# Turning the rows after the first norm by a transposing DMA instead of on TensorE, in an attention and ternary-FFN layer

## The chip, the cores and the metric

The kernel runs on one core of a Trainium2 chip. A core has five engines that run their own instruction lists in order and meet at semaphores: TensorE (PE, matrix products; its weight loads are shown as PEld), VectorE (DVE), ScalarE (ACT), GpSimd (POOL) and SyncE (SP), whose queue issues nearly all transfers here. Transfers run on 16 DMA engines. TensorE writes its results to PSUM; everything else works on SBUF, and DVE and ACT also read PSUM. The metric is the device time of one execution in microseconds (us).

## The reference

The layer takes `x` of 8 sequences of 1024 tokens with 512 features, and does linear attention with random features, a residual and a norm, then a layer with ternary weights, a residual and a norm:

```
def feature_map(x, orf):
    proj = x @ orf.T / d_k ** 0.25
    norm = jnp.sum(x * x, axis=-1, keepdims=True) / (2.0 * math.sqrt(d_k))
    return (jnp.exp(proj - norm) + EPS) / math.sqrt(m)
q = feature_map(split(x @ Wq.T + bq), orf)       # 16 heads of 32, 128 features each
k = feature_map(split(x @ Wk.T + bk), orf)
v = split(x @ Wv.T + bv)
kv = jnp.einsum('nlm,nld->nmd', k, v)
ksum = jnp.sum(k, axis=1)
...
out = out[..., :-1] / out[..., -1:]
x = _layernorm(x + out @ Wo.T + bo)              # the first norm
w_ternary = ste_quantize(weight)                 # -1, 0, 1
x = _layernorm(x + einsum('bsi,oi->bso', x, w_ternary * scale))
```

All is float32. The kernel keeps float32 accuracy from float16 matmuls by splitting a value into two float16 parts, a high part and the remainder.

## The kernel before, in words

The 8192 tokens go in 16 blocks of 512 (TB), two to a sequence; a block has four row tiles of 128 tokens (`tt`), and the 512 features have four groups of 128 (`kt` or `i`).

A block passes through these stages. `X` loads the transposed input (`xraw`) and splits it (`xh` on ACT, `xl` on DVE). `Stacked.project` makes k or q on PE, clamps it on DVE, and splits it on ACT and DVE into `part`; SP stores the parts to DRAM (`ds`) and loads them back in another layout (`st`, lines 576 and 577, and the norms `dn` to `st`, line 581). `KBlock.feature` multiplies `st_k` with the random features (`kf_ps`, line 630), ACT takes the exponent (`e`, line 635), POOL sums it, and PE accumulates `kvt`. `QBlock.feature` does the same for q (`qf_ps`, line 779); `products` makes numerator and denominator (`num_ps`, `den`, line 798, narrow matmuls into 32 output partitions each). The denominator (`rd` on ACT) goes to DRAM (`dd`, line 822), is inverted and is spread back (`r`, `dr`, `rb`). `divide` gives `oh` and `ol`, and `attn` multiplies them with Wo (`o_ps`, line 368).

Then comes the part that the change touches. For each row tile, `attn_add` (line 937, DVE) adds `o_ps` into the residual `y`; `layernorm` takes moments on DVE, the power on POOL, the shift on DVE, and applies both on ACT in place (line 904). `turn` (line 949) transposes the normed tile on PE, four float32 transposes of 128x128 into one PSUM tile `x_tp`. `x1_high` (line 953, ACT) reads that PSUM tile, scales it and writes the high float16 part `x1h`; `x1_low` (line 957, DVE) reads the PSUM tile and `x1h` and writes the remainder `x1l`. `ffn` (line 972) multiplies both parts with the ternary weights, eight matmuls to a row tile; `ffn_add`, the second norm and the store follow.

The order of the work is written out by hand. Class `Order` takes steps: a PE step has a place on a time axis and a length; a step of another engine has a delay behind a PE step (`after`) or a place (`at`); each lists what it needs. `emit` sorts all steps by the times that follow from this, lets narrow PE steps (`tiled`) be drawn together within a window, and issues the instructions in that order. Each engine then runs its own list in order, so places set nothing but the order on each engine; what waits is decided on the chip. The numbers in the code (`units`, the places of a block, the delays) are these places.

Buffers matter too: a tag with so many buffers is a ring, and a new tile waits until the last user of the tile that it replaces is done. PSUM tiles of tag `pj` have six buffers, `x1h` and `x1l` four each. Tag `t3`, three buffers of 2 KB a partition, holds `rd` of each block and, once per sequence, `kvt` and `kst`.

## Time and profile before

| What | Value |
|---|---|
| median of 3 runs | 1205.96 us (1203.72 to 1206.58) |
| the profiled execution's own time | 1203.99 us |
| its span, first to last instruction | 1202.1 us |
| granted TensorE clock | 0.997 of full speed |
| PE busy | 1174.0 us, 98% |
| DVE, ACT, POOL busy | 71%, 68%, 44% |
| DMA queue of SP | 166.24 MB, 48.2% of 16 engines |

Busy time is the union of an engine's instructions. PE's matmuls overlap, so the mean length of one is longer than the time from one start to the next; what a matmul costs PE is read from starts. In a group's line the part behind the bar is busy time and mean ns of one, and behind the second bar the engine's idle time just before and what ended it. In a line of the order of time the first number is the start, the second the length, and `x8` counts merged instructions. `SPq` is SP's queue, where the length is the time of issuing, not that of the transfer. In a table of stages the clock, the DMA engines' share and GB/s stand at the end of a line.

### The profile page before, as it was taken

To read this page: it belongs to the slowest core of one execution; us is meant where nothing else is said; L and a number is where in the kernel's file an instruction comes from. 1 tells how busy PE (TensorE), PEld (TensorE's weight loads), DVE (VectorE), ACT (ScalarE), POOL (GpSimd) and SP (SyncE) were. 2 spreads that over 40 slices of the span, in tenths; PEclk is the share of its full clock that TensorE was granted. 3 is DMA by queue.
4 is the path that set the end of the run, shared out by engine and by line. 5 is a ranking of instruction groups with operands and counts; after the bars stand their busy time and mean duration, and the time that the engine had idled before them with its cause. 6 is when DMAs were issued, how large, how long until landed. Compare 5 with 4: busy or idle time off the path is not lost.

```text
span 1202.1 us, 23702 instructions
## 1 busy us (share of the span) xinstructions
PE 1174.0 (98%) x8732; PEld 578.2 (48%) x8732; DVE 848.6 (71%) x1726; ACT 821.6 (68%) x1377; POOL 534.6 (44%) x485
## 2 busy tenths in 40 slices
PE   7899999999999999999999999999999999999996
PEld 4455454545445454554545445454544545445333
DVE  7886776776767676686766857578675776747488
ACT  4677686685766857676685766856677676857744
POOL 0357254615455253642527435273444625455323
PEclk9999999999999999999999999999999999999999
DMA  5556365453645436354454645536354453545621
GB/s 172 164 153 188 96 175 148 137 169 83 191 119 156 144 105 191 89 175 135 129 165 106 187 118 147 153 102 195 87 169 136 137 170 81 173 115 160 171 74 70
DMA packets 94819, 169.38 MB, mean 141 GB/s; under 512 B 14736, under 2 KB 48624, under 8 KB 92656
## 3 DMA queue, kind: packets, MB, share of 16 engines
q1 hardware_dynamic: 93296, 166.24, 48.2%
q10 hardware_dynamic: 1408, 1.63, 0.4%
q8 instruction: 69, 1.13, 0.4%
q14 instruction: 46, 0.38, 0.1%
HBM read 108.06 MB, written 59.77 MB: 140 GB/s over the span
## 4 chain that ended last, share of the span: by engine, by line
PE 85%; DVE 9%; ACT 3%; DMA 2%; issue 1%; POOL 0%; SPq 0%; ACTq 0%; POOLq 0%
PE q_ps L355 13%; PE v_ps L368 13%; PE k_ps L355 12%; PE o_ps L368 11%; PE f_ps L972 8%; PE kvt_ps L664 5%; PE kf_ps L630 5%; PE num_ps L798 5%; PE den L798 4%; PE qf_ps L779 4%; PE x_tp L949 2%; PE n_ps_k L545 1%; DMA y<-in_x_dram 1%; PE n_ps_q L545 1%; ACT qf L783 1%; DVE k_ps L497 1%
## 5 line engine op out<-in xcount | busy, mean ns | idle before, releaser
L647 POOL TENSOR_TENSOR esum<-esum,e 128x512 f32<-128x512 f32 x192 | 255.3, 1331 | 138.6 <-ACT e L635 130.8
L635 ACT ACTIVATE e<-kf_ps 128x512 f32<-128x512 f32 x256 | 149.8, 599 | 118.3 <-PE kf_ps L630 94.4
L783 ACT ACTIVATE qf<-qf_ps 128x512 f32<-128x512 f32 x256 | 141.6, 610 | 27.5 <-PE qf_ps L779 27.3
L928 POOL TENSOR_TENSOR y<-y,bo_sb 128x512 f32<-128x512 f32 x64 | 83.6, 1313 | 126.1 <-DMA y<-in_x_dram 58.5
L894 POOL TENSOR_TENSOR rs_a<-ve_a,neg_half 128x1 f32<-128x1 f32 x64 | 35.1, 548 | 194.8 <-DVE ve_a L889 172.6
L630 PEld LDWEIGHTS <-st_k 98*128 98x128 f16 x1024 | 75.9, 97 | 62.9 <-issue 12.9
L630 PE MATMUL kf_ps<-of,st_k 98*128 98x128 f16 x1024 | 96.2, 219 | 1.5 <-ACT e L635 1.2
L937 DVE SCALAR_TENSOR_TENSOR y<-o_ps,odown,y 128x512 f32<-128x512 f32 x64 | 47.9, 748 | 66.1 <-PE o_ps L368 65.5
L606 DVE SCALAR_TENSOR_TENSOR v<-v_ps,down_kqv,bv_sb 128x512 f32<-128x512 f32 x60 | 44.6, 744 | 62.3 <-PE v_ps L368 62.2
L779 PE MATMUL qf_ps<-st_q,of 98*128 98x512 f16 x256 | 82.2, 380 | 0.2
L368 PEld LDWEIGHTS <-oh 128*128 128x128 f16 x512 | 49.1, 97 | 67.0 <-ACT oh L871 7.3
L337 ACT ACTIVATE xh<-xraw,xup 128x512 f16<-128x512 f32 x64 | 45.2, 715 | 51.6 <-DVE xup L231 51.6
L355 PEld LDWEIGHTS <-wh_k 128*128 128x128 f16 x512 | 49.7, 99 | 59.7 <-issue 4.9
L510 DVE SCALAR_TENSOR_TENSOR rest_q<-q_ps,down_kqv,part_q 128x512 f32<-128x512 f32 x60 | 44.9, 748 | 46.7 <-ACT sq_q L505 44.6
L904 ACT ACTIVATE y<-y,mr_a,rs_a 128x512 f32<-128x512 f32 x64 | 52.4, 818 | 36.8 <-DVE mr_a L898 36.1
L618 POOL TENSOR_TENSOR vsum<-vsum,v 128x512 f32<-128x512 f32 x48 | 65.9, 1374 | 21.7 <-DVE v L606 21.6
L894 POOL TENSOR_TENSOR rs_f<-ve_f,neg_half 128x1 f32<-128x1 f32 x64 | 44.5, 695 | 67.8 <-DVE ve_f L889 63.4
L368 PEld LDWEIGHTS <-xh 128*128 128x128 f16 x512 | 48.5, 98 | 49.9 <-issue 3.4
L368 PE MATMUL o_ps<-wh_o,oh 128*128 128x512 f16 x256 | 67.1, 379 | 3.3 <-ACT oh L871 2.5
L355 PEld LDWEIGHTS <-wh_q 128*128 128x128 f16 x512 | 47.1, 97 | 45.5 <-issue 0.4
L368 PE MATMUL o_ps<-wh_o,ol 128*128 128x512 f16 x256 | 66.5, 378 | 2.0 <-DVE ol L876 2.0
L798 PE MATMUL num_ps<-qf,kv 128*32 128x512 f32 x512 | 67.4, 596 | 0.2
(216 smaller groups left out, 2715.0 us busy)
## 6 DMA issues: line engine op xcount, KB each, us to landing
ds_k<-part_k SPq DMA_DIRECT2D x128, 128.0 KB
st_k<-ds_k SPq DMA_DIRECT2D x64, 256.0 KB
ds_q<-part_q SPq DMA_DIRECT2D x128, 128.0 KB
st_q<-ds_q SPq DMA_DIRECT2D x64, 256.0 KB
rb<-dr SPq DMA_DIRECT2D x64, 256.0 KB
y<-in_x_dram SPq DMA_DIRECT2D x64, 256.0 KB
out_dram<-y SPq DMA_DIRECT2D x64, 256.0 KB
xraw<-in_xT_dram SPq DMA_DIRECT2D x15, 1024.0 KB
```

The lines of the kernel that those rows point to most:

```text
L355: nc.tensor.matmul(ps, a[:, kt, c], b[kt], start=(n == 0), stop=(n == 3 * KT - 1))
L368: nc.tensor.matmul(ps, a[kt][:, c], wt[:, kt, :], start=(n == 0), stop=(n == 3 * KT - 1))
L618: nc.gpsimd.tensor_tensor(sums["v"], sums["v"], vs[tt], op=ALU.add)
L630: nc.tensor.matmul(ps[:, j, :], self.st[i][0:NF, j, c], of, start=True, stop=True)
L635: nc.scalar.activation(e, self.eps[i, tt], AF.Exp, scale=EXP_SCALE)
L647: nc.gpsimd.tensor_tensor(es, before, self.es[i, tt].rearrange("p j m -> p (j m)"), op=ALU.add)
L779: nc.tensor.matmul(self.qps[n], of, self.st[i][0:NF, j, :], start=True, stop=True)
L783: nc.scalar.activation(e, self.qps[n], AF.Exp, scale=EXP_SCALE)
L798: nc.tensor.matmul(to[DK * j : DK * (j + 1), :], kvl[:, n, i * P + DK * j : i * P + DK * (j + 1)], self.qf[i, j], start=first, stop=last, ...
L894: nc.gpsimd.tensor_tensor(self.rs[name], self.ve[name], neg_half, op=ALU.pow)
L928: nc.gpsimd.tensor_tensor(y, y, bo_sb, op=ALU.add)
L972: nc.tensor.matmul(ps, a[:, kt, :], tern.w[:, kt, :], start=(n == 0), stop=(n == 2 * KT - 1))
```

## The change

The turned float16 parts are made in another order. After the norm is applied, `x1_high` and `x1_low` split the row tile `y` itself, in SBUF, into the two halves of a tile `x1p` (128 x 2 x 512, float16, tag `t3` with its three buffers). SP then issues one transposing DMA for the tile, which writes `x1t` (128 x 8 x 128, four buffers). `ffn` reads the eight 128x128 pieces of `x1t`. The four transposes on PE and the PSUM tile are gone. `turned` is no longer a PE step with a place of its own: it hangs behind the output's PE step with delays, called from `output`.

Nearly all other places and delays in the order also have new numbers, without changing what is computed.

```
-        def turn(self, tt):
-            self.tps[tt] = pj.tile([P, KT, P], F32, tag="pj", name=f"x1_tp_{self.t}_{tt}")
-            for kt in range(KT):
-                nc.tensor.transpose(self.tps[tt][:, kt, :], self.y[tt][:, kt * P : (kt + 1) * P], ident)
-        def x1_high(self, tt):
-            self.x1h[tt] = sb.tile([P, KT, P], F16, tag="x1h", name=f"x1h_{self.t}_{tt}", bufs=4)
-            nc.scalar.mul(self.x1h[tt], self.tps[tt], X1_SCALE)
-        def x1_low(self, tt):
-            xl = sb.tile([P, KT, P], F16, tag="x1l", name=f"x1l_{self.t}_{tt}", bufs=4)
-            nc.vector.scalar_tensor_tensor(
-                xl, self.tps[tt], X1_SCALE, self.x1h[tt], op0=ALU.mult, op1=ALU.subtract
-            )
-        def turned(self, tt, place):
-            step = pe(place, 0.45, self.turn, tt, needs=[self.a_gates[tt]])
-            high = after(step, 2.07, self.x1_high, tt)
-            self.x1_gates[tt] = after(step, 5.07, self.x1_low, tt, needs=[high])
+            self.turned(tt, step)                      # at the end of output
+        def x1_high(self, tt):
+            self.x1p[tt] = sb.tile([P, 2, D], F16, tag="t3", name=f"x1p_{self.t}_{tt}", bufs=3)
+            nc.scalar.mul(self.x1p[tt][:, 0, :], self.y[tt], X1_SCALE)
+        def x1_low(self, tt):
+            pair = self.x1p[tt]
+            nc.vector.scalar_tensor_tensor(
+                pair[:, 1, :], self.y[tt], X1_SCALE, pair[:, 0, :], op0=ALU.mult, op1=ALU.subtract
+            )
+        def turn(self, tt):
+            self.x1t[tt] = sb.tile([P, 2 * KT, P], F16, tag="x1t", name=f"x1t_{self.t}_{tt}", bufs=4)
+            nc.sync.dma_start_transpose(self.x1t[tt], self.x1p[tt].rearrange("p a d -> p (a d)"))
+        def turned(self, tt, step):
+            high = after(step, 2.06, self.x1_high, tt, needs=[self.a_gates[tt]])
+            low = after(step, 9.26, self.x1_low, tt, needs=[high])
+            self.x1_gates[tt] = after(step, 3.37, self.turn, tt, needs=[low])
...
-            for a in self.x1t[tt]:
+            for a in range(2):
                 for kt in range(KT):
-                    nc.tensor.matmul(ps, a[:, kt, :], tern.w[:, kt, :], start=(n == 0), stop=(n == 2 * KT - 1))
+                    nc.tensor.matmul(ps, self.x1t[tt][:, KT * a + kt, :], tern.w[:, kt, :], start=(n == 0), stop=(n == 2 * KT - 1))
...
-    units = [0.0, 51.61, 104.67, 168.51]
+    units = [0.0, 51.61, 104.84, 168.05]
...
-        k.norms(a + k0 + (19.92 if t > 2 else 3.7))
+        k.norms(a + k0 + (16.46 if t > 2 else 2.9))
...
-        y, r, m, d, f = u + -5.46, u + 13.45, u + -5.65, u + 12.58, u + 42.82
-        ys, rs, ms, fs, ds = 6.01, 0.05, 5.86, 5.63, 2.42
+        y, r, m, d, f = u + -4.0, u + 9.12, u + -5.65, u + 14.73, u + 42.82
+        ys, rs, ms, fs, ds = 5.43, 1.72, 5.86, 5.08, 3.06
...
-            f = E + (45.81, 87.24, 112.69)[n]
+            f = E + (44.62, 85.21, 115.19)[n]
```

## The prediction

> **What bounds the kernel now.** I read the page's engine shares first, then the table of stages, then the groups with shapes kept apart, then the order of time on PE and on SP's queue in one steady block.
>
> The page's first part, and the table of stages (us; then PE, PEld, DVE, ACT, POOL busy with counts; clock; DMA share; GB/s):
>
> ```profile
> PE 1174.0 (98%) x8732; PEld 578.2 (48%) x8732; DVE 848.6 (71%) x1726; ACT 821.6 (68%) x1377; POOL 534.6 (44%) x485
> ...
> q1 hardware_dynamic: 93296, 166.24, 48.2%
> ```
> ```profile
> 180.00:1102.00 922.00, 919.20 (x6947) 452.36 (x6945) 637.56 (x1285) 642.17 (x1082) 427.52 (x379) 1.00 0.49 140
> ...
> 1162.00:1202.00 40.00, 29.20 (x146) 14.36 (x144) 33.89 (x86) 18.39 (x27) 12.62 (x18) 0.94 0.14 53
> ```
>
> From 180 to 1102 us PE is idle 2.8 us in 922, at full clock: what leaves PE's list there shortens the kernel, if nothing new makes PE wait. In the last 40 us PE is busy 29 and DVE 34; the chain of waits there is mostly DVE (moments, the two adds, x1l). PE work that leaves there is worth nothing; DVE work added there costs its length.
>
> Groups by shape (busy us, mean ns of one | idle before): the removed transposes, the two splits that move, and the nearest rows for what they become.
>
> ```profile
> L949 PE MATMUL x_tp<-ident,y 128*128 128x128 f32 x256 | 36.7, 273 | 0.1
> L957 DVE SCALAR_TENSOR_TENSOR x1l<-x_tp,x1h 128x512 f16<-128x512 f32 x64 | 42.6, 681 | 6.5 <-ACT x1h L953 6.4
> L953 ACT ACTIVATE x1h<-x_tp 128x512 f16<-128x512 f32 x64 | 37.8, 629 | 1.1 <-PE f_ps L972 1.1
> L343 DVE SCALAR_TENSOR_TENSOR xl<-xraw,xup,xh 128x512 f16<-128x512 f32 x64 | 59.2, 933 | 2.0 <-ACT xh L337 2.0
> L876 DVE TENSOR_TENSOR ol<-num,oh 128x512 f16<-128x512 f32 x64 | 46.8, 739 | 4.8 <-ACT oh L871 4.8
> L871 ACT CAST oh<-num 128x512 f16<-128x512 f32 x64 | 39.6, 621 | 27.3 <-DVE num L866 27.2
> L337 ACT ACTIVATE xh<-xraw,xup 128x512 f16<-128x512 f32 x64 | 45.2, 715 | 51.6 <-DVE xup L231 51.6
> ```
>
> Order of time in block 11, PE (start us, length): where eight transposes stand, and what follows them.
>
> ```profile
> 771.61 1.04 PE L949 MATMUL x_tp<-ident,y 128*128 128x128 f32 x8
> 772.58 1.06 PE L798 MATMUL num_ps<-qf,kv 128*32 128x512 f32 x8
> 773.46 1.04 PE L798 MATMUL den<-qf,kv 128*32 128x512 f32 x8
> ...
> 775.18 1.04 PE L798 MATMUL den<-qf,kv 128*32 128x512 f32 x8
> 776.15 0.62 PE L630 MATMUL kf_ps<-of,st_k 98*128 98x128 f16 x8
> 776.61 0.61 PE L949 MATMUL x_tp<-ident,y 128*128 128x128 f32 x4
> 777.05 0.39 PE L630 MATMUL kf_ps<-of,st_k 98*128 98x128 f16 x4
> ```
>
> Matmuls overlap, so starts count: four transposes from 776.61 to 777.05 take 0.44 us, 109 ns each, not the mean of 273. Before a narrow (128*32) group eight take 0.97 instead of 0.87: entering narrow work costs 0.10. Between narrow groups eight take 0.86 to 0.88, but the last before kf_ps 0.97: leaving costs another 0.10.
>
> SP's queue in the same block:
>
> ```profile
> 767.67 0.33 SPq L562 DMA_DIRECT2D dn_k<-n_k  x1
> 773.17 0.25 SPq L581 DMA_DIRECT2D st_k<-dn_k  x1
> 773.52 0.50 SPq L576 DMA_DIRECT2D st_k<-ds_k  x1
> ...
> 774.70 0.27 SPq L581 DMA_DIRECT2D st_k<-dn_k  x1
> ...
> 780.35 0.34 SPq L827 DMA_DIRECT2D r<-dd  x1
> 785.38 0.34 SPq L837 DMA_DIRECT2D dr<-r  x1
> 786.85 1.72 SPq L843 DMA_DIRECT2D rb<-dr  x4
> ```
>
> One issue holds SP 0.25 to 0.6 us, and between issues SP sits waiting. This is the room that the new transfers get.
>
> **The change, part by part.**
>
> *Transposes leave PE.* 64 turns of four, 0.436 us each: 27.9 us. Eight turns start after 1162, in the DVE-bound tail, and count nothing. The other 56 give −24.4 (ends −24.4 and −27.9). 64 PSUM tiles go too; PE hardly waits for PSUM (0.1 us before x_tp), so nothing for that.
>
> *PE's new order.* In the built programs PE's list has 74 stretches of narrow matmuls before and 93 after. 19 more at 0.10 + 0.10 = +3.9 us (down to +2 if half of the borders fall where PE waits anyway).
>
> *The split moves ahead of the turn.* x1_high now reads y in SBUF: 621 (oh) to 715 (xh) ns for 629; ACT gets −0.5 to +5.5 us in all, at 68% busy, covered by PE. x1_low reads SBUF twice: 739 (ol, same shapes, one operation less) to 933 (xl, the same two operations) for 681. I take 933: DVE +16 us in all, 0.25 each, covered at 71% busy. In the tail eight of them are not covered: +2 (low end +0.5). If DVE's cover went, the 16 us would appear, less the tail's 2.
>
> *The transposing DMA, 64 of 256 KB, all on SP's queue.* No row shows one. As bytes it adds 16.8 MB to 166.2 MB: the 48.2% share of the DMA engines becomes 53%. At the page's rate (166.24 MB in 48.2% of 1202 us, 287 GB/s) one takes 0.9 us of the DMA engines and, like a plain 256 KB load, 0.5 us of SP. The other end: the instruction as built moves blocks of 16 rows, so a partition gets 32 bytes of a block; if each such piece cost a mean packet (0.482 x 16 x 1202 us over 93296 packets, 99 ns), one takes 8192 / 16 x 99 ns = 51 us, and 64 take 3.2 ms. The ends lie far apart; I take the plain 256 KB load as the nearest row, because the transfer moves whole rows of one tile, doubled for caution: about 2 us of SP and of the rings.
>
> Where it stands: in a steady block SP's list now reads x1t_0, three loads of st_k_1, x1t_1, x1t_2, st_k_2, x1t_3, st_k_3, the stores of dd. Each x1t waits for x1_low on DVE, and all of that queues behind it. Who waits: kf_ps on PE for st_k. In the block shown st_k_1's last load is issued at 774.70 and its first matmul starts at 781.40; st_k_0's last load, at 773.17, is read at 776.15, so about 3.0 us suffice to land and 3.4 us are spare. st_k_2 and st_k_3 have 10 us more and over (read at 792.9 and 802.7). k's norms also move 3.5 us earlier, which puts st_k_0 ahead of x1t_0. The consumer has the most room: f_ps starts 16 to 24 us after x1l's end in steady blocks (771.3 to 787.3 and the like). ACT gets one real new wait: x1p shares three buffers with rd, so x1p_3 waits for x1t_0's landing, and rd for x1t_1's. The applies of rows 0 and 3 are 11.3 us apart (763.86, 775.19): x1t_0 has some 9 us. At 2 us all of this is covered: 0. In the tail the last rows' f_ps came 0.4 to 1.0 us after x1l; now a landing lies between. By dd to r (last dd issued by 778.52, r at 780.35) that is 1.8 us or more; DVE has other rows' work meanwhile: +1 (0 to +4).
>
> *New places elsewhere* (SP, ACT, POOL and DVE lists all reshuffled). PE idles 28 us in all, 10.8 of them in the last 40, about 11 in the first 60, under 4 between 60 and 1102. There is little to win and I take −4, with ends −8 and +8.
>
> Sum: −24.4 + 3.9 + 2 + 0 + 1 − 4 = −21.5. The profiled execution took 1203.99 us (span 1202.1, 1.9 around it), 2.0 below the median of 1205.96. So 1182.5, and 1184 against the median.
>
> [...]
>
> **The rivals.**
>
> *Hidden (likeliest), 0.56.* 1184, own range 1172 to 1197.
>
> *The transposes back up SP's queue: slower, 0.31.* SP's waits in the block shown, 768.0 to 773.17, 780.7 to 785.38 and 788.57 to 792.79, with st_k_1's 3.4 us, are about 17 to 18 us of room for four: it decides from 4.5 us of queue per transpose. Beyond it st_k comes late, kf_ps waits, ACT stalls in x1p_3, and each further us costs four times in some 14 blocks, 56 us. At 5 us 1212, at 6 us 1268, at 7 us 1324; at 51 us over 4 ms. For it: nothing in the trace moves data in 2-byte steps, and SP waited 5.2 us for one 256 KB store (767.67 to 773.17), so the rings are not idle. Against: SP's small room is needed only if the price is nine times a plain issue.
>
> *Hidden, but the gain is eaten, 0.13.* DVE's uncovered part (14), the worse places (+8) and landings in the tail (+4) together give back 10 to 26: 1194 to 1210. For: 19 more narrow stretches. Against: DVE at 71%.
>
> **How the numbers follow.** 0.3% (3.6 us) is about what a measurement of this kernel can tell from no change. Faster: 0.56 and 0.05 of the last, 0.61. Same: 0.05. Slower: 0.31 and 0.03, 0.34. Range: below, the hidden case with all 27.9 and places −8, 1170. Above, up to 6.1 us per transpose, 1275, which leaves about 0.15 above it and 0.02 below.
>
> **What would show it.** Right: no x_tp on PE; PE busy near 1150; 64 issues x1t<-x1p on SP of 2 us or less; kf_ps waiting for st_k no more than now; x1p ahead of x1t by one DVE step; DVE x1l near 0.93 us; the last f_ps 2 to 4 us behind their x1l. Wrong: issues or landings of x1t over 4.5 us, PE waiting for st_k or f_ps for x1t in every block, ACT idle before x1p_3 or rd.

## The result and the profile after

The changed kernel takes 1215.33 us (median of 4 runs, 1212.36 to 1215.76), the kernel before on the same chip 1204.90. The ratio is 1.008, with a 95% interval of 1.0058 to 1.0102: 10 us slower, where 21.5 us less were forecast. The profiled execution has a span of 1213.9 us.

Three lines of the page of the changed kernel: busy time by engine, packets, and SP's queue.

```profile
PE 1161.1 (96%) x8476; PEld 549.2 (45%) x8476; DVE 865.7 (71%) x1726; ACT 832.2 (69%) x1377; POOL 529.7 (44%) x485
...
DMA packets 162402, 186.14 MB, mean 153 GB/s; under 512 B 82320, under 2 KB 116208, under 8 KB 160240
...
q1 hardware_dynamic: 160880, 183.03, 61.3%
```

The 256 transposes have left PE's list (8732 to 8476), and 16.8 MB more cross SP's queue, as forecast. The queue's packets went up by 67,584, that is 1056 for each of the 64 transfers, most of them of 256 bytes, and its share of the DMA engines went from 48.2% to 61.3%. Worked out: (0.613 x 1213.9 - 0.482 x 1202.1) / 64 = 2.6 us of all 16 engines for one transfer.

The stages of the changed kernel (us; PE, PEld, DVE, ACT, POOL busy; clock; DMA share; GB/s):

```profile
60.00:180.00 120.00, 111.54 (x986) 56.41 (x975) 78.45 (x137) 83.29 (x140) 58.38 (x45) 0.97 0.48 138
180.00:1102.00 922.00, 909.42 (x6707) 427.92 (x6705) 653.11 (x1279) 653.99 (x1086) 426.04 (x382) 1.00 0.65 155
1102.00:1162.00 60.00, 54.61 (x371) 21.73 (x368) 41.83 (x87) 40.05 (x70) 18.00 (x20) 0.97 0.66 166
1162.00:1214.00 52.00, 36.00 (x152) 14.70 (x152) 42.22 (x107) 22.74 (x32) 16.49 (x21) 0.90 0.50 122
```

PE's idle time between 180 and 1102 us is 12.6 us, where it was 2.8; between 60 and 180 us it is 8.5, where it was 0.5 in the kernel before:

```profile
60.00:180.00 120.00, 119.47 (x1035) 60.36 (x1024) 87.81 (x145) 91.04 (x154) 63.36 (x47) 1.00 0.53 153
```

The changed kernel's groups with shapes kept apart:

```profile
L953 DVE SCALAR_TENSOR_TENSOR x1p<-y,x1p 128x512 f16<-128x512 f32 x64 | 45.8, 715 | 0.3 <-ACT x1p L949 0.3
L949 ACT ACTIVATE x1p<-y 128x512 f16<-128x512 f32 x64 | 40.3, 630 | 3.2 <-DMA x1t<-x1p 1.2
L630 PE MATMUL kf_ps<-of,st_k 98*128 98x128 f16 x1024 | 97.2, 219 | 16.4 <-DMA st_k<-ds_k 8.0 <-DVE x1p L953 4.5 <-DMA st_k<-dn_k 1.7
```

The two splits are cheap in SBUF. The new wait is that of `kf_ps` (16.4 us idle ahead of it). From block 3 to block 14 it comes once in a block, at the first `kf_ps`, which reads `st_k_0` (0.1 us in block 5, 0.5 to 1.9 us in the others); where the view names `x1p` or another tile of DVE, it is the same place. Block 11 of the changed kernel in order of time, first SP's queue, then PE (start, length):

```profile
771.70 0.51 SPq L301 DMA_DIRECT2D xraw<-in_xT_dram  x1
772.32 0.50 SPq L576 DMA_DIRECT2D st_k<-ds_k  x1
772.87 0.57 SPq L577 DMA_DIRECT2D st_k<-ds_k  x1
774.99 0.26 SPq L581 DMA_DIRECT2D st_k<-dn_k  x1
775.29 0.54 SPq L527 DMA_DIRECT2D ds_k<-part_k  x1
775.92 2.99 SPq L960 DMA_TRANSPOSE x1t<-x1p  x1
...
781.33 4.39 SPq L960 DMA_TRANSPOSE x1t<-x1p  x2
```
```profile
783.16 0.38 PE L630 MATMUL kf_ps<-of,st_k 98*128 98x128 f16 x4 [1.05 <-DMA st_k<-ds_k]
```

`st_k_0` was asked for at 772.32 and 772.87, ahead of the block's first transpose at 775.92, and at 783.16 PE has waited 1.05 us for it. The issue of one transpose takes SP 1.23 us at the least, 1.82 on the mean over all 64, and 2.99 here.

The records of packets and landings tell what happens meanwhile. A spill `ds_k` lands in four parts, 5.2 to 5.9 us behind its issue (medians of 128; one more record comes at 1.0 us), where a load of `st_k` lands in 16. Around 770.5 us, where little else runs, four or five packets, all of 1024 bytes, are under way at a time. Both are read here as a spill on 4 of the 16 DMA engines. From 780 to 782.5 us at least 16 packets are under way all the time, yet only 0.03 to 0.04 MB move in each half microsecond. Beside the packets of a spill and a few of 4 and 8 KB these are 256-byte packets of the transpose, 18 ns long at the median; 16 of them last over 1 us, up to 4.2, and end together at 782.9. Of the 16 landings of `st_k_0`'s second load four come between 779.59 and 781.52, and twelve between 782.95 and 783.03, right behind that end.

So it is in each of the twelve blocks from 3 to 14: 15 to 20 long packets of the transpose end together, `st_k_0`'s last part lands 0.1 to 0.5 us later, and `kf_ps` starts within 0.13 us of that. The waits at these twelve places add up to 11.7 of the 16.4 us. Over all 64 transposes the 16 landings of one lie within 0.15 us of each other at the median. For a plain copy of the same bytes (`e3_plain_copy` below) they lie 2.8 us apart. These records look as if the parts of a transpose waited for each other, and a load that was issued ahead waited with them. What holds either, no run shows.

A gap of PE can have a price of its own. Two stretches of the changed kernel around a wait of 3.62 us for ACT (columns as above), and PE's line:

```profile
172.40:176.00 3.60, 0.04 (x4) 0.04 (x6) 1.25 (x2) 1.21 (x3) 0.00 (x0) 0.99 0.97 260
176.00:179.40 3.40, 3.40 (x15) 1.20 (x16) 3.40 (x6) 3.03 (x6) 1.81 (x1) 0.51 0.69 199
```
```profile
175.96 0.65 PE L664 MATMUL kvt_ps<-e,v 128*32 128x128 f32 x8 [3.62 <-ACT e L635]
```

After the gap the granted clock is 0.51 for 3.4 us, which costs, as an estimate from these two numbers, some 1.7 us more. The same follows a wait of 1.98 us that ends at 100.0. It does not follow every wait: behind one of 1.90 us that ends at 495.9 the clock stays up. Between 60 and 1180 us the changed kernel has four such stretches, the kernel before none.

### The profile page after: what moved, and what is told of

Read it like the earlier page. It is cut to its first block, busy times and chain, and to the rows that moved or that the text cites. A ratio compares the mean times of both kernels' runs of the same rounds, so it can differ in the third digit from the quotient of the medians.

```text
span 1213.9 us, 23180 instructions
## 1 busy us (share of the span) xinstructions
PE 1161.1 (96%) x8476; PEld 549.2 (45%) x8476; DVE 865.7 (71%) x1726; ACT 832.2 (69%) x1377; POOL 529.7 (44%) x485
## 3 DMA queue, kind: packets, MB, share of 16 engines
q1 hardware_dynamic: 160880, 183.03, 61.3%
## 4 chain that ended last, share of the span: by engine, by line
PE 77%; DVE 11%; DMA 7%; ACT 2%; issue 1%; POOL 1%; SPq 1%; POOLq 0%; DVEq 0%; ACTq 0%
PE q_ps L355 12%; PE v_ps L368 11%; PE k_ps L355 11%; PE o_ps L368 11%; PE f_ps L972 8%; PE kf_ps L630 4%; PE kvt_ps L664 4%; PE num_ps L798 4%; DMA st_k<-ds_k 4%; PE den L798 4%; PE qf_ps L779 3%; PE n_ps_k L545 1%; PE n_ps_q L545 1%; DMA rb<-dr 1%; DVE num L866 1%
## 5 line engine op out<-in xcount | busy, mean ns | idle before, releaser
L647 POOL TENSOR_TENSOR esum<-esum,e 128x512 f32<-128x512 f32 x192 | 251.4, 1313 | 154.9 <-ACT e L635 152.2
L783 ACT ACTIVATE qf<-qf_ps 128x512 f32<-128x512 f32 x256 | 146.4, 603 | 32.5 <-PE qf_ps L779 32.0
L972 PE MATMUL f_ps<-tern,x1t 128*128 128x512 f16 x512 | 128.7, 379 | 1.3 <-DMA x1t<-x1p 0.5
L894 POOL TENSOR_TENSOR rs_a<-ve_a,neg_half 128x1 f32<-128x1 f32 x64 | 41.3, 646 | 180.7 <-DVE ve_a L889 180.6
L630 PE MATMUL kf_ps<-of,st_k 98*128 98x128 f16 x1024 | 97.2, 219 | 16.4 <-DMA st_k<-ds_k 8.0
L779 PE MATMUL qf_ps<-st_q,of 98*128 98x512 f16 x256 | 88.1, 382 | 2.5 <-DVE st_f L885 1.5
L618 POOL TENSOR_TENSOR vsum<-vsum,v 128x512 f32<-128x512 f32 x48 | 62.0, 1292 | 30.0 <-DVE xm L210 17.0
L972 PEld LDWEIGHTS <-x1t 128*128 128x128 f16 x512 | 47.3, 98 | 61.3 <-issue 8.1
L504 ACT ACTIVATE part_k<-k_ps,bk_sb,down_kqv 128x512 f16<-128x512 f32 x60 | 46.9, 782 | 35.0 <-DVE k_ps L497 25.8
```

What stands on the lines that cost most here:

```text
L618: nc.gpsimd.tensor_tensor(sums["v"], sums["v"], vs[tt], op=ALU.add)
L630: nc.tensor.matmul(ps[:, j, :], self.st[i][0:NF, j, c], of, start=True, stop=True)
L647: nc.gpsimd.tensor_tensor(es, before, self.es[i, tt].rearrange("p j m -> p (j m)"), op=ALU.add)
L779: nc.tensor.matmul(self.qps[n], of, self.st[i][0:NF, j, :], start=True, stop=True)
L783: nc.scalar.activation(e, self.qps[n], AF.Exp, scale=EXP_SCALE)
L894: nc.gpsimd.tensor_tensor(self.rs[name], self.ve[name], neg_half, op=ALU.pow)
```

## The experiments

The theories of the first round were: A, the new places cost the time; B, the transposing DMA does. In several kernels x1 stays unturned or sums are left incomplete, so that a cost can be taken out; each is named where it comes. "Old" and "new" places are those of the kernel before and of the changed kernel.

### Each part alone

`e1_old_places` is the kernel before, with the new splits and the transposing DMA hung behind the output step:

```
             self.a_gates[tt] = self.layernorm(step, last, tt, f"a_{self.t}_{tt}")
+            self.turned(tt, step)
...
-            q.turned(tt, d + ds * tt + 15.51)
```

> The transposing DMA and the split ahead of it as in the changed kernel, but every other step at the place it had in the kernel before. Theory A (the new places cost the time: the longer start-up, kf_ps waiting at 93 to 176 us, and the tail; the transposing DMA itself is as good as hidden): the 25 us less of PE work come through, 1180 to 1190 us. Theory B (the transposing DMA costs the time: it holds SP's queue and all 16 DMA engines in front of st_k's loads, and kf_ps waits in every block): 1205 to 1220 us, with kf_ps waiting for st_k some 1 to 2 us per block at the old places too.

Measured: 1236.3 us, ratio 1.0275 (1.0238 to 1.0313). Neither theory: the old places make it worse. The waits of this kernel that stand out (us in total, times, longest):

```profile
ACT x1p L949 <- DMA x1t<-x1p: 15.1, 11, 3.2
PE kvt_ps L664 <- ACT e L635: 13.4, 13, 2.4
```

Here the ring of three `x1p` fills: ACT waits for a landing of `x1t` before it may write the next `x1p`, and what stands behind it in ACT's list, `e`, comes late for PE. `e6_spread_old_places` below shows that this is not all: there the wait for `x1t` is gone and that of `kvt_ps` is not.

`e2_new_places` keeps the transposes on TensorE and puts all else at the new places:

```
-            self.turned(tt, step)
...
+            q.turned(tt, d + ds * tt + 15.51)
```

> The transposes on TensorE and the split behind them as in the kernel before, with every other step at the places of the changed kernel. Theory A (places): PE's work is back (+25) and the places' waits stay (some 11 us before 180 us, some 10 in the last 100): 1222 to 1236 us. Theory B (transposing DMA): the places are worth nothing much either way, 1200 to 1212 us, and the waits of kf_ps for st_k in the steady blocks are gone.

Measured: 1267.6 us, ratio 1.0521 (1.05 to 1.0543), far outside of both. The turns on PE need places of their own, which the new places don't have, and the ones chosen here may be bad ones. So this run doesn't price the new places. It does say that the numbers of an order belong to one list of work.

### The transposing DMA, step by step

`e3_plain_copy` moves the same bytes with a plain DMA, and `e11_no_dma` lets the splits write into `x1t` itself. In both x1 is not turned, and the second matmul of a block reads unturned rows.

```
-            nc.sync.dma_start_transpose(self.x1t[tt], self.x1p[tt].rearrange("p a d -> p (a d)"))
+            nc.sync.dma_start(self.x1t[tt].rearrange("p a d -> p (a d)"), self.x1p[tt].rearrange("p a d -> p (a d)"))
```
```
-            self.x1p[tt] = sb.tile([P, 2, D], F16, tag="t3", name=f"x1p_{self.t}_{tt}", bufs=3)
+            self.x1t[tt] = sb.tile([P, 2 * KT, P], F16, tag="x1t", name=f"x1t_{self.t}_{tt}", bufs=4)
+            self.x1p[tt] = self.x1t[tt].rearrange("p (a k) d -> p a (k d)", a=2)
...
-            self.x1_gates[tt] = after(step, 3.37, self.turn, tt, needs=[low])
+            self.x1_gates[tt] = low
```

> The changed kernel with a plain DMA of the same 256 KB from x1p to x1t in place of the transposing one; x1 is not turned, so the second matmul of the block multiplies the unturned rows. Theory A (places): nothing changes, 1210 to 1217 us. Theory B (what is costly is the transposing form: 1.24 us of SP each, 1024 packets of 256 bytes, all 16 engines held until the slowest is through): the 14 us that the steady blocks lost come back and part of the tail's, 1194 to 1202 us, and kf_ps waits for st_k in the steady blocks no more than before (under 0.5 us per block).

> The changed kernel with no DMA between x1p and x1t: the two splits write into x1t itself, and x1 is not turned. Spills on 4 engines. It gives the time without any transfer. Theory C: like the plain copy or a little below it, 1190 to 1200 us; what is then left above 1182 us (the 25 us less of PE work) is the new places' own. Theory A in its weaker form (the places also cost some 20 us): 1200 to 1210 us.

Measured: 1202.1 us (ratio 0.9977, 0.9963 to 0.9992) and 1202.2 us (0.9986, 0.9966 to 1.0005). A plain copy of 256 KB a row tile costs nothing that these runs can tell; the transposing form costs 13 us. Theory C's range for the kernel without any transfer, 1190 to 1200 us, is missed: it lies where the weaker form of theory A put it, so the transposing DMA is not all that keeps the kernel from the forecast 1184 us. The wait of `kf_ps` without any DMA falls from 16.4 to 5.2 us:

```profile
L630 PE MATMUL kf_ps<-of,st_k 98*128 98x128 f16 x1024 | 97.0, 218 | 5.2 <-DMA st_k<-dn_k 3.3 <-ACT e L635 0.9 <-DVE x1t L954 0.8
```

`e4_spread_after` is the changed kernel with spills that land in 16 parts. The DRAM tile gets the shape of the SBUF tile, so that the outermost dimension of the store is 128 and not 4, and the load takes the new layout apart. The loads thereby become three in place of two, and no run parts this from the stores:

```
-                self.ds[i] = dram.tile([2, DK, HPT, TB], F16, tag="ds", name=f"ds_{self.which}_{self.t}_{i}")
-            nc.sync.dma_start(self.ds[i][r].rearrange("d j t -> j d t"), self.part[i][:, r, :])
+                self.ds[i] = dram.tile([2, P, TB], F16, tag="ds", name=f"ds_{self.which}_{self.t}_{i}")
+            nc.sync.dma_start(self.ds[i][r], self.part[i][:, r, :])
...
-            ds = self.ds[i].rearrange("r d j t -> (r d) j t")
-            nc.sync.dma_start(st[0 : 2 * DK], ds)
-            nc.sync.dma_start(st[2 * DK : 3 * DK], ds[DK : 2 * DK])
+            for n, r in enumerate((0, 1, 1)):
+                nc.sync.dma_start(st[n * DK : (n + 1) * DK], self.ds[i][r].rearrange("(j d) t -> d j t", d=DK))
```

> The changed kernel with k's and q's spilled parts stored from 128 partitions in a layout that reaches all 16 DMA engines, where the present store uses 4 of them, and loaded back in three loads of 32 partitions. Theory A (places): little changes, 1208 to 1218 us. Theory B in the form that a transposing DMA waits on the 4 engines that hold the spills' backlog, and holds the other 12 meanwhile: without the backlog kf_ps no longer waits for st_k in the steady blocks, 1196 to 1206 us. Theory B in the form that the issue on SP alone delays the loads: no change, or slower by the third load's issue (0.5 us on SP for each of 128 stacks, covered or not): 1212 to 1225 us.

Measured: 1194.02 us, ratio 0.991 (0.9895 to 0.9925). This is 21 us less than the changed kernel and 11 less than the kernel before. Between 180 and 1102 us PE is busy as it was before the change, and `kf_ps` no longer waits for its loads:

```profile
180.00:1102.00 922.00, 919.36 (x6836) 434.42 (x6838) 672.56 (x1315) 663.19 (x1103) 432.32 (x387) 1.00 0.63 159
```
```profile
L629 PE MATMUL kf_ps<-of,st_k 98*128 98x128 f16 x1024 | 97.0, 218 | 1.2 <-ACT e L634 0.9 <-DVE ve_a L888 0.3
```

The old spills, with an outermost dimension of 4, land in four parts, the spread ones, with 128, in 16.

Four more kernels part the spread from the transposing DMA. `e5_spread_before` has the same spread in the kernel before, `e10_plain_spread` has it with the plain copy (x1 unturned), `e16_spread_k_only` has it for k alone, and `e18_no_dma_spread_k` for k alone with no DMA (x1 unturned). In the two for k alone both pairs of lines above are chosen by

```
+            ds = self.ds[i][r] if self.which == "k" else self.ds[i][r].rearrange("d j t -> j d t")
+            nc.sync.dma_start(ds, self.part[i][:, r, :])
```

> The kernel before with the spills stored from 128 partitions over all 16 DMA engines, as in the run that took the changed kernel to 1194 us. Theory C (only a transposing DMA suffers from spills that sit on 4 engines, because it holds the other 12 until these are through): in the kernel before, where kf_ps did not wait for st_k, nothing is won, 1200 to 1208 us. Theory D (spills on 4 engines cost time in either kernel): 1183 to 1192 us, and the gain of the spread says nothing about the transposes.

> The changed kernel with spread spills and with a plain DMA from x1p to x1t in place of the transposing one (x1 is not turned). Theory C: without a backlog the transposing form costs little more than a plain copy, 1188 to 1194 us against 1194 us. If the form itself (1.24 us of SP, 1024 packets of 256 bytes) costs time without a backlog too: 1175 to 1186 us.

> The changed kernel with only k's spills spread over 16 engines; q's keep their 4 engines and their two loads. The transposes stand on SP's queue between k's spills and st_k's loads, q's spills come some 30 us after them. If the backlog of k's spills is what the transposes wait on: all of the gain is here, 1188 to 1196 us, and with 64 loads fewer than with both spread perhaps a little below its 1194 us. If the spread helps for another reason (shorter stores, or loads in other pieces, for k and q alike): about half of the gain, 1202 to 1208 us.

> The changed kernel with no DMA between x1p and x1t (1202 us), with k's spills spread over 16 engines. If k's spills hinder the new places also without any transposing DMA: 1192 to 1197 us, the same as with the transposing DMA and the same spread (1196.8), so that the transfer costs nothing there. If the spread only undoes what the transposing DMA suffers: 1200 to 1204 us.

Measured: 1211.2 (ratio 1.0046, 1.0032 to 1.006), 1195.3 (0.9911, 0.9893 to 0.9929), 1196.8 (0.9928, 0.9912 to 0.9945) and 1197.2 us (0.9932, 0.9917 to 0.9947). The kernel before gains nothing from the spread and loses 6 us, so theory D falls; it lies above theory C's range (1200 to 1208) as well, and what loses the 6 us was not looked into. In the changed kernel the spread of k alone gives 18.5 of the 21 us. With it, the transposing DMA (1196.8) costs no more than no DMA at all (1197.2), and with both spread no more than a plain copy (1194.0 against 1195.3). Theory C holds in this: the 13 us exist only together with k's spills in the old layout, which land in four parts. The spread also gives the new places 5 us without any transfer, which C did not say.

`e12_act_queue` issues the transposes from ACT's queue:

```
-            nc.sync.dma_start_transpose(self.x1t[tt], self.x1p[tt].rearrange("p a d -> p (a d)"))
+            nc.scalar.dma_start_transpose(self.x1t[tt], self.x1p[tt].rearrange("p a d -> p (a d)"))
```

> The changed kernel with the transposes issued from ACT's queue in place of SP's; spills on 4 engines. Theory C says that what costs is that a transpose stands behind the spills in the order of one queue and st_k's loads behind it. From another queue its packets need not wait for the spills, nor st_k's loads for it: kf_ps waits for st_k under 5 us in all (16 us by line in the changed kernel), 1196 to 1208 us, ACT's 64 issues of 1.24 us included as far as PE covers them. If it is the DMA engines themselves that are held, whatever the queue, kf_ps waits as before and ACT's 79 us of issues come on top: 1215 to 1250 us.

Measured: 1266.4 us, ratio 1.0498 (1.0457 to 1.0539). From the page and the groups of this kernel:

```profile
q1 hardware_dynamic: 93296, 166.24, 47.9%
q10 hardware_dynamic: 68992, 18.42, 11.0%
```
```profile
L630 PE MATMUL kf_ps<-of,st_k 98*128 98x128 f16 x1024 | 100.8, 224 | 4.7 <-DMA st_k<-dn_k 1.9 <-ACT sq_q L505 1.5 <-ACT e L635 0.9
L779 PE MATMUL qf_ps<-st_q,of 98*128 98x512 f16 x256 | 93.8, 394 | 37.6 <-ACT num L810 22.8 <-ACT qf L783 13.7 <-DMA st_q<-dn_q 0.8
```

Half of what C expects is there: from a queue of their own the transposes leave `kf_ps` 4.7 us of idle time and not 16.4. But ACT now issues each transpose itself, 1.43 us on the mean, behind DVE's `x1p`, and `qf_ps` is idle 37.6 us, 36.5 of them for ACT. The time lies outside of both ranges, so this run tells only where the wait of `kf_ps` comes from.

### The old places with the DMA

> The transposing DMA at the old places (1236 us), with the spills over 16 engines. There ACT's x1p waited 15 us for landings of x1t (11 times), and PE's kvt_ps and v_ps for ACT's e behind it (25 us). Theory C (the landings are late because the transposes wait behind the spills' backlog): the waits go, 1178 to 1195 us. Theory E (the rows come too close together there for a ring of three x1p shared with rd, whatever the DMA engines hold): ACT's wait for x1t stays over 10 us, 1215 to 1236 us.

`e6_spread_old_places` is `e1_old_places` with the spread. Measured: 1221.2 us, ratio 1.0128 (1.0105 to 1.0151). ACT's wait for `x1t` goes from 15.1 to 1.3 us, as theory C says; PE's wait of `kvt_ps` for `e` stays at 12.1 us (13.4 in `e1_old_places`), so the time doesn't follow. It falls into theory E's range, but without E's wait: neither theory explains it.

`e19_old_splits` and `e20_old_splits_spread_k` put the splits at their old places too, and the DMA right behind them:

```
+        def turned(self, tt, place):
+            high = at(place + 2.07, self.x1_high, tt, needs=[self.a_gates[tt]])
+            low = at(place + 5.07, self.x1_low, tt, needs=[high])
+            self.x1_gates[tt] = at(place + 5.08, self.turn, tt, needs=[low])
```

> The old places for every step, the two splits too (they read y in SBUF), and the transposing DMA directly behind the low part. x1p is held some 4 us before its DMA, not 7 as with the changed kernel's delays at the old places (1236 us). Spills on 4 engines. If holding x1p in a ring of three was what made ACT wait there: 1195 to 1210 us, less the better the hold of the DMA engines is hidden. If the transposing DMA hurts at the old places in any case: 1215 to 1240 us.

> The same with k's spills spread over 16 engines. If old places, short hold and spread spills together keep what the removed PE work is worth: 1180 to 1192 us, faster than the changed kernel with the spread (1194). If the gain at the old places is small anyway: 1194 to 1210 us.

Measured: 1258.6 (ratio 1.0422, 1.0381 to 1.0464) and 1246.0 us (1.0327, 1.03 to 1.0354). Both lie outside of their ranges. A shorter hold of `x1p` is no cure; ACT still waits 11.8 and 20.4 us for `x1t`, and `f_ps` now waits 9.5 and 7.7 us for it as well. Why the old places carry the DMA so badly stays open.

### What the transposes on PE were worth

`e17_turn_removed` is the kernel before without the transposes, and with nothing in their place: the splits read `y` at the places that the order had given them, and x1 is not turned.

```
-            step = pe(place, 0.45, self.turn, tt, needs=[self.a_gates[tt]])
-            high = after(step, 2.07, self.x1_high, tt)
-            self.x1_gates[tt] = after(step, 5.07, self.x1_low, tt, needs=[high])
+            high = at(place + 2.07, self.x1_high, tt, needs=[self.a_gates[tt]])
+            self.x1_gates[tt] = at(place + 5.07, self.x1_low, tt, needs=[high])
...
-            q.turned(tt, d + ds * tt + 15.51)
+            q.turned(tt, d + ds * tt + 15.96)
```

> The kernel before with the transposes on TensorE left out and nothing in their place: the two splits read y in SBUF, at the places that they had; x1 is not turned. It gives what 27.9 us less of PE work are worth with the old places. If the prediction's first step was right (24.4 us of it on the path): 1178 to 1184 us. If much of it was not on the path, because PE then runs into waits for other engines that the transposes had covered: 1190 to 1200 us.

Measured: 1203.86 us, ratio 0.999 (0.998 to 0.9999), above both ranges. All transposes are gone, nothing replaces them, and 1.5 us are won. In block 11 of the kernel before, the eight transposes stood between the last six `qf_ps` and the `num_ps` and `den` which read what ACT makes of them. Its order of time, the line of PE ahead of those shown in the prediction, and ACT's:

```profile
770.31 1.46 PE L779 MATMUL qf_ps<-st_q,of 98*128 98x512 f16 x6
```
```profile
770.79 3.04 ACT L783 ACTIVATE qf<-qf_ps 128x512 f32<-128x512 f32 x6
773.67 1.15 ACT L953 ACTIVATE x1h<-x_tp 128x512 f16<-128x512 f32 x2
```

And the same piece of both lists without the transposes:

```profile
768.35 1.46 PE L779 MATMUL qf_ps<-st_q,of 98*128 98x512 f16 x6
769.74 1.35 PE L798 MATMUL num_ps<-qf,kv 128*32 128x512 f32 x8
770.63 1.33 PE L798 MATMUL den<-qf,kv 128*32 128x512 f32 x8
771.49 1.65 PE L798 MATMUL num_ps<-qf,kv 128*32 128x512 f32 x7
772.52 0.63 PE L798 MATMUL den<-qf,kv 128*32 128x512 f32 x3
772.97 0.59 PE L798 MATMUL num_ps<-qf,kv 128*32 128x512 f32 x1
772.97 1.44 PE L798 MATMUL den<-qf,kv 128*32 128x512 f32 x5
774.35 0.84 PE L630 MATMUL kf_ps<-of,st_k 98*128 98x128 f16 x12
```
```profile
767.34 0.62 ACT L948 ACTIVATE x1h<-y 128x512 f16<-128x512 f32 x1
...
768.91 2.55 ACT L783 ACTIVATE qf<-qf_ps 128x512 f32<-128x512 f32 x5
771.29 0.69 ACT L948 ACTIVATE x1h<-y 128x512 f16<-128x512 f32 x1
771.81 0.65 ACT L783 ACTIVATE qf<-qf_ps 128x512 f32<-128x512 f32 x1
```

From the first of the six `qf_ps` to the `kf_ps` behind the group it was 770.31 to 776.15, 5.84 us, with eight transposes in it; it is 768.35 to 774.35, 6.00 us, without them. `num_ps` and `den` stretch from 3.57 us (772.58 to 776.15) to 4.61, because they wait for ACT: the last `qf` ends at 772.46, and the `num_ps` that reads it starts at 772.51.

Two causes are mixed in these 1.04 us. One is cover: in the kernel before, PE worked off transposes while ACT caught up. The other is that this run also changed ACT's list: without the PE step that they had hung behind, two `x1h` now stand ahead of the last `qf`, where the kernel before had both behind it. Counted from the first of the six `qf_ps`, the last `qf` ends 3.52 us later in the kernel before and 4.11 us later here. These 0.59 us are ACT's own delay, and by this estimate the cover is the other 0.45. All twelve groups of this kind between 180 and 1102 us are longer by 1.04 to 1.18 us, and all have two `x1h` ahead. A run with the `x1h` kept behind `qf` would part the two causes; there is none.

The waiting can be counted over the whole kernel. For each pair of neighbouring matmuls the start-to-start time that such a pair takes at the lower quartile in the kernel before stands for PE at work, and the rest is waiting. PE at work falls by 27 to 30 us, by how the narrow matmuls are grouped, and the waiting rises by as much. Between 180 and 1102 us some 13 us of the rise lie at `num_ps` and `den`, and some 10 at `kvt_ps`, which reads ACT's `e`.

DVE slowed down too. The group of `xl` in this kernel, 933 ns on the mean in the kernel before:

```profile
L343 DVE SCALAR_TENSOR_TENSOR xl<-xraw,xup,xh 128x512 f16<-128x512 f32 x64 | 70.1, 1104 | 0.0
```

By its overlap with POOL in the trace, `xl` takes 745 ns on the mean where POOL is idle, and 1355 ns (741 to 1821) where POOL is busy for over 90% of it; 36 of 64 fall into the second kind, where 18 did in the kernel before. Why it takes longer beside POOL, no run shows. To see what this is worth, `e21_removed_less_pool` cuts most of POOL's adds to 64 of 512 columns, which leaves the sums of e incomplete, and `e22_before_less_pool` does the same to the kernel before.

```
+            if self.half == 1 or tt > 1:
+                es, before, new = es[:, 0:64], before[:, 0:64], new[:, 0:64]
```

> The old places with the transposes left out (1203.9 us), and 160 of POOL's 192 adds of e cut from 512 columns to 64, so that POOL is busy far less; the sums of e are not complete. Theory F: at the old places the gain is lost because PE's shorter list shifts DVE's two-input instructions onto POOL's work, where each takes 1.1 to 1.4 us and not 0.68 to 0.74 (xl 933 to 1104 ns on the mean, DVE 39 us more in all), and PE then waits for what ACT and DVE make. With POOL mostly quiet the gain must come out: 1178 to 1190 us, xl near 800 ns. If the gain is lost for another reason: 1198 to 1206 us.

> The kernel before with the same cut of POOL's adds, for comparison. PE is busy 98% there and idle some 6 us between 60 and 1102 us, so a faster DVE has little to give: 1198 to 1206 us by either theory. If this falls as far as the other run, the cut and not the removed transposes is what is seen there.

Measured: 1198.5 (ratio 0.9944, 0.9929 to 0.9959) and 1204.8 us (0.9997, 0.9987 to 1.0006). `xl` falls to 793 ns, as theory F expects:

```profile
L343 DVE SCALAR_TENSOR_TENSOR xl<-xraw,xup,xh 128x512 f16<-128x512 f32 x64 | 50.3, 793 | 0.0
```

But only 5.4 us come back, against some 20 that F asks for, and the waiting at `kvt_ps` falls by as much. F is a part. The 13 us at `num_ps` and `den` are unchanged in this run.

The old places are not those of the changed kernel, and there the loss lies elsewhere. The start of block 4's first `kf_ps`, the time from there to that of block 14, and the rest, in the profiled executions:

| us | up to block 4 | ten blocks | from block 14 on |
|---|---|---|---|
| before | 271.4 | 722.8 | 207.9 |
| `e17_turn_removed`, old places, no transposes | 272.8 | 718.4 | 211.0 |
| `e11_no_dma`, new places, no transfer | 273.4 | 713.1 | 212.3 |
| `e18_no_dma_spread_k`, the same, k's spills spread | 271.2 | 708.9 | 214.7 |
| `e16_spread_k_only`, the same with the transposing DMA | 270.8 | 708.9 | 214.5 |
| changed kernel | 279.9 | 720.0 | 214.0 |

The ten blocks had 40 of the 64 turns, 17.4 us, and have 15 of the 19 new narrow stretches, 3.0 us: by the prediction's own figures they should gain 14.4, and 17.4 at the old places, where no stretches are new. They gain 4.4 at the old places, 9.7 at the new ones without a transfer, and 13.9 with k's spills spread, whether the rows are turned by the DMA or not turned at all. So at the new places, and with k's spills spread, the removed work is worth in the steady blocks what was forecast. It is the start and the end that give nothing, or give back: with `e16_spread_k_only` PE is idle 3.2 us more up to block 4 and 4.9 us more from block 14 on than in the kernel before, and four stretches of 3.4 us at half the clock lie between 60 and 1180 us.

### The ends

With the spread, `o_ps` still waits 4.5 us for ACT's `oh` in the last blocks, and the start has its gaps. `e13_spread_old_tail` takes the old places for the last blocks, `e14_spread_old_start` for the weights and the first blocks, both on top of the spread; the diffs are those places of the change, turned around, such as

```
-                k.close([end + 74.81, end + 73.24, end + 81.56], s)
+                k.close([end + 74.49, end + 66.45, end + 80.11], s)
```
```
-    units = [0.0, 51.61, 104.84, 168.05]
+    units = [0.0, 51.61, 104.67, 168.51]
```

> The changed kernel with spread spills (1194 us), the last blocks' steps at the places of the kernel before. There o_ps waits some 12 us between 1102 and 1162 us, where the kernel before waited 3. If the new places of the last blocks are what costs that: 1184 to 1190 us. If the transposing DMA's landings cost it at any places: 1192 to 1202 us.

> The changed kernel with spread spills (1194 us), the weights' and the first blocks' steps at the places of the kernel before. The first kf_ps of block 4 came at 268.2 us with the new places and spread spills, against 271.4 before, where 6.3 us less of PE work had been counted up to there. If the new places of the start cost the rest: 1188 to 1192 us. If not: 1193 to 1200 us.

Measured: 1198.4 (ratio 0.9943, 0.9928 to 0.9958) and 1198.1 us (0.9939, 0.9922 to 0.9955), both 4 us above the new places. Theory A falls at both ends: the new places are the better ones there, given the new list of work. What else would mend the ends stays open.

### All in one table

| us | old places | new places |
|---|---|---|
| transposes on PE | 1204.9 | 1267.6 (turns at places chosen for the run) |
| the same, spills spread | 1211.2 | |
| x1 unturned, no transfer | 1203.9 | 1202.2 |
| the same, k's spills spread | | 1197.2 |
| plain copy | | 1202.1; spread 1195.3 |
| transposing DMA | 1236.3; splits at old places 1258.6 | 1215.3 |
| the same, k's spills spread | splits at old places 1246.0 | 1196.8 |
| the same, all spills spread | 1221.2 | 1194.0 |

The best kernel is the changed one with all spills spread: 1194.0 us, 0.9% below the kernel before.

## Why the prediction was wrong

*Transposes leave PE, -24.4.* This step failed. At the old places the transposes left out, with nothing put in, are worth 1.5 us; in the changed kernel without any transfer, new places included, 2.7 us (1204.9 to 1202.2). The instructions were counted rightly: PE at work falls by 27 to 30 us in the first of these kernels and by 23 to 28 in the second, by the count above, where 27.9 and, less 3.9 for the borders, 24.0 were forecast. What was wrong is to take "PE is idle 2.8 us in 922: what leaves PE's list there shortens the kernel, if nothing new makes PE wait" for a price without looking for the new waits. At the old places they open where the transposes stood, and the prediction's own fence showed the place: `x_tp` directly ahead of `num_ps`, which reads what ACT makes of the `qf_ps` before it. How much of that is cover, and how much the order of ACT's list in that run, is an estimate, about half and half. At the new places the ten steady blocks gain 9.7 of the 14.4 us that fall to them, and 13.9 with k's spills spread; the start and the end, where 16 of the 56 counted turns lie, lose 6.4 us to new waits of PE instead of gaining.

*PE's new order, +3.9.* The order has 93 narrow stretches as counted. The count of PE at work is too coarse to price the borders; in the ten blocks 17.4 us of turns and a gain of 13.9 leave 3.5, near the 3.0 forecast for their borders.

*The split ahead of the turn.* `x1_high` is 630 ns, inside its bounds. `x1_low` was mis-sized: 715 ns, not 933. The row of `ol` was the nearer one, and the 933 of `xl` were, as is known now, the mean of an instruction that runs beside POOL for over 90% of its length in 18 of 64 cases.

*The transposing DMA, 0.* This step failed as well, by 13 us. The price of one was about right: SP 1.23 us at the least and 1.82 on the mean, 2.6 us of the DMA engines, for 2 us taken. From issue to last landing it is no slower than the plain copy (4.2 us at the median, 5.2 for the plain copy), but it takes more time of the engines: the plain copy takes (0.539 x 1200.6 - 0.482 x 1202.1) / 64 = 1.06 us of them. The difference is mostly packets that last far longer than the median: 1024 packets at the median of 18 ns would be, as an estimate, 1.2 us of 16 engines.

What failed is the conclusion from price to cost. The prediction looked at how long SP is held and who queues behind it, found 3.4 us of room for `st_k_1`, and gave `st_k_0`, which goes out ahead of `x1t_0`, no price. It is `st_k_0` that PE waits for, block after block. The rival of the backed-up queue was to decide from 4.5 us of queue per transpose, and the loss came at 1.8, because it doesn't show in SP's issues but in the landings: the transpose's long packets end together, at 782.9 in block 11, and the last parts of `st_k_0` land only behind them, up to 783.03. That a spill of k, still running, keeps the transpose back fits the runs with the spread; the trace does not show the hold itself. The prediction had the hint, SP's wait of 5.2 us for one 256 KB store, and used it only as "the rings are not idle". The late landings are seen in twelve blocks; that k's spills in the old layout are the other half of the cost is shown by the runs. About half of the cost falls ahead of block 4 (273.4 to 279.9 us in the profiled executions).

*Landings in the tail, +1.* `f_ps` waits 0.5 us for `x1t`, and of the last stretch's new waits the largest, 3.2 us, is `o_ps` waiting for ACT's `oh`. What makes `oh` late there, or PE early, no run shows.

*New places, -4.* With no transfer in either kernel the medians are 1203.9 and 1202.2 us, ratios of 0.999 and 0.9986 whose intervals overlap, so as a whole the new places can't be told from nothing. In the profiled executions they win 5.3 us in the ten steady blocks and lose 1.9 at the two ends. The prediction had them act on waits that the kernel before had; they act on waits that the missing transposes open.

So, in the runs' own terms: -1.5 for the transposes at the old places, -1.7 for the new places (not clear of noise), +13.1 for the transposing DMA, +9.9 in all against 10.4 measured. The first two act on each other, and the run with the transposes at the new places (1267.6) doesn't price them the other way round. The prediction's range of 1170 to 1275 us holds the time, its likeliest case does not. Its third rival, "hidden, but the gain is eaten", came nearest in kind, at 1194 to 1210; it lacked the transposing DMA's 13 us. What it named as a sign of being wrong, PE waiting for `st_k` in block after block, is what the profile shows first. One of its sums is off: 51 us a transpose, at 56 us for each beyond 4.5, give 3.8 ms and not over 4; nothing rests on it.

## What to carry to other kernels

A matmul that leaves a busy PE is worth its time only if the next one in the list is ready without it. Before counting such work as a gain, look at what stands on either side: if the two sides depend on each other through another engine, the work between them is in part cover, and the other engines' lists have to be laid out anew. Look at the steady blocks and at the start and the end apart: here the one gained what was forecast, with the spills spread, and the others gave back nearly half of it.

Before a transposing DMA is put on a queue, see in how many parts the transfers around it land, those ahead of it too, and spread them first: here k's spills in four parts and the 64 transposes cost 13 us together, and with the spills spread the transposes cost nothing that the runs can tell. Leaving a transfer out, or putting a plain copy in its place, tells in two runs what it costs and which part of it. And when a step is left out to see what it was worth, compare the order of every other engine's list before reading the time.

## What the runs showed of the hardware that was not expected

- The 16 parts of a transposing DMA of 256 KB land within 0.15 us of each other (median of 64), those of a plain copy within 2.8 us. With k's spills landing in four parts beside them, 64 transposing DMAs cost the kernel 13 us and 64 plain ones nothing; with these spills spread, 1196.8 us stand against 1197.2 without any transfer.
- A load of `st_k` that was issued ahead of a transposing DMA had its last part land 0.1 to 0.5 us behind the end of that DMA's long packets, in each of twelve blocks.
- `xl`, a DVE instruction with two SBUF inputs, takes 743 to 745 ns on the mean while POOL is idle, and 1169 (kernel before) and 1355 ns (`e17_turn_removed`) where POOL is busy for over 90% of it. Leaving PE's transposes out changed how many of them meet POOL, and DVE's busy time by 39 us, with no DVE instruction added; a part of it is `x1l`, which reads SBUF twice there (681 to 763 ns on the mean).
- In the changed kernel waits of PE of 1.55, 1.98, 3.23 and 3.62 us were each followed, within 1.4 us, by 3.4 us at half the clock; waits of 1.53, 1.62 and 1.90 us were not.
